# Order of shifts and scores within a head attention step

## The chip, the cores and the metric

The kernel runs on one core of a Trainium2 chip. The time is device time in microseconds of one execution. TensorE (PE) does the matrix products, ScalarE (ACT) the exponentials and copies, VectorE (DVE) maxima and sums, GpSimd (POOL) sums of pairs and casts, SyncE (SP) issues the transfers.

## The reference

Eight batch elements, each with 1024 rows of 512 numbers and a context of 1024 rows of 384. Two gated residual blocks follow each other; the first is cross attention with 8 heads of 64 (here: kind 1), the second self attention with 16 heads of 32 and a gate on each row (kind 2).

```python
q = (x @ Wq).reshape(B, Nq, HEADS, DIM_HEAD)             # kind 1, k and v from the context
sim = jnp.einsum('bihd,bjhd->bhij', q, k) * SCALE
attn = jax.nn.softmax(sim, axis=-1)
out = jnp.einsum('bhij,bjhd->bihd', attn, v)
...
q_scaled = (q_norm + query_embedding[None]) * jax.nn.softplus(temperature)[None]   # kind 2
attn = jnp.einsum('bhqd,bhkd->bhqk', q_scaled, k) / math.sqrt(hd)
attn = jax.nn.softmax(attn, axis=-1)
h = jnp.einsum('bhqk,bhkd->bhqd', attn, v)
...
x = x + jnp.tanh(g_xattn[0]) * _L0_xattn_ref(_layernorm(x), ...)
x = x + jnp.tanh(g_ffn[0]) * _L0_ffn_ref(_layernorm(x), ...)
```

## The kernel before

Batch elements are worked one after the other. For each element and kind the heads go in four chunks of 128 rows (class `Chunk`): two heads of 64 rows in kind 1, four heads of 32 rows in kind 2. The rows of q and k that belong to one head sit on that head's rows of TensorE's array, so the products of different heads of a chunk use different row groups.

A chunk passes through three stages, which overlap with those of its neighbours. `project` makes q and k. `maxima` (L373) computes scores once in bf16 into tiles `pm` and takes their row maxima on VectorE (L421, or L404 where two banks go at once); the negated maxima are turned to rows `sh` by a transfer. `attention` (L590) then goes over the steps (h, s): h is one half of 512 queries, s runs over four pairs of key blocks (kind 1) or eight key blocks (kind 2). With four chunks, two halves and eight elements there are 256 steps of kind 1 and 512 of kind 2.

A step is made by `score` (L445) and `value` (L549). `score` fills two PSUM tiles `sc` of two banks each, so four banks in all. Bank j gets two products, summed in PSUM: the shift, a product of a row of ones with a row of `sh` (m == 0, bf16, one row of the array), and the score, k times q (m == 1, fp32). In kind 2 the four banks belong to the four heads, on four different row groups: tile 0 has heads 0 and 1, tile 1 heads 2 and 3. ScalarE then takes the exponential of each tile into a tile `e` (L473). `value` multiplies `e` with v into the tile `av` (L560); these products use all rows of the array and 32 or 64 of its columns. GpSimd and VectorE add up `e` tiles (L478, L491) for the sums (L511).

The pool `ps_sc` has two buffers, so a step's tile can be written only when the exponential of the step before has read the same buffer. The score of step m + 1 is issued before the value of step m. The variable `order` says which tile comes first; in kind 2 it is turned round when the maxima pair just issued (`taken`) uses the rows of heads 0 and 1:

```python
order = (1, 0) if taken[0] and self.kind == 2 else (0, 1)
...
for m in range(2):
    for j in (2 * u + v for u in order for v in range(2)):
```

[...]`attend` (L679) fills in maxima and projections between scores and values by planned times (`pe`, `dve`, `pool`, with `self.SC` 1250 ns for a kind-2 score step). These planned times don't depend on the order within `score`.

Of the kernel before, what the change touches and what calls it, by code (L numbers as in the profile page):

```python
# [21 lines left out]
def tile_gated_block(  # L22
# [38 lines left out]
    nc = tc.nc  # L61
# [172 lines left out]
    def pe(ns):  # L234
        at["PE"] += ns
# [27 lines left out]
    class Chunk:  # L263
# [181 lines left out]
        def score(self, step):  # L445

            h, s = step
            nh, width, key = self.nh, self.width, self.key  # L450
            order = (1, 0) if taken[0] and self.kind == 2 else (0, 1)
            taken[0] = False
            pss = {
                u: ps_sc.tile([P, 2, H], F32, tag="sc", name=f"sc_{key}_{h}_{s}_{u}") for u in order
            }
            for m in range(2):
                for j in (2 * u + v for u in order for v in range(2)):
                    kk, i = divmod(j, nh)
                    r, kc = i * width, s * self.nk + kk
                    if m == 0:  # L460
                        r += kk * HD2
                        lhsT, rhs = ones_b[r : r + 1, :], self.sh[r : r + 1, ts(h, H)]
                    else:
                        rows = slice(r, r + width)
                        lhsT, rhs = self.k[rows, ts(kc, P)], self.q[rows, ts(h, H)]
                    nc.tensor.matmul(  # L466
                        pss[j // 2][:, j % 2, :], lhsT=lhsT, rhs=rhs, start=(m == 0), stop=(m == 1)
                    )
            pe(self.SC)
            e = {}  # L470
            for u in order:
                e[u] = epool.tile([P, 2, H], F32, tag="e", name=f"e_{key}_{h}_{s}_{u}")
                nc.scalar.activation(e[u], pss[u], AF.Exp)  # L473
            self.e[step] = e
# [639 lines left out]
```

## Time and profile before

| | |
|---|---|
| median of 3 runs | 4967.27 us (4964.01 to 4967.46) |
| profiled execution | 4964.66 us, span 4962.6 us |
| granted TensorE clock | 0.998 |
| TensorE busy | 4751.6 us (96%) |
| VectorE busy | 3126.6 us (63%) |
| GpSimd busy | 2571.3 us (52%) |
| ScalarE busy | 2307.6 us (47%) |
| scores sc<-q,k L466 | 6144 matmuls, 1114.5 us busy |
| shifts sc<-sh,ones_b L466 | 3072 matmuls, 408.2 us busy, 99.9 us idle before |
| exponentials e<-sc L473 | 1536, 1491.1 us busy, mean 1021 ns |

A line of the timeline gives the start and length in us of neighbouring instructions of one kind, the engine, the line of the kernel, what is written and read, how many, and in brackets the engine's idle time before them with what ended it. PEld are TensorE's weight loads. A matmul's end is modelled: its row is longer than the time for which it holds its rows of the array, so starts are compared with starts. A wait for several semaphores is put down to the one that came last.

### The profile page before, as it was taken

Reading aid. Unit: us, or ns where it says so; the run is one execution under the profiler, and the core shown is the slowest. Engines: PE = TensorE matmul, PEld = TensorE weight load, DVE = VectorE, ACT = ScalarE, POOL = GpSimd, SP = SyncE. Lnnn points to the kernel's source line nnn. Section 1 sums busy time; section 2 is a strip of 40 time slices with the busy share of each in tenths; the row PEclk is TensorE's granted clock in tenths of the full one; section 3 lists DMA queues with packets and bytes.
Section 4 is the critical chain, followed back from the end, with each engine's and each line's share of the span. In section 5 each row is a group of like instructions: output and inputs, shape, how many; then the busy total and the mean of one; then the engine's idle time right before and its main releaser. Section 6 shows DMA issues by size and latency. Waiting matters only on the chain.

```text
span 4962.6 us, 83502 instructions
## 1 busy us (share of the span) xinstructions
PE 4751.6 (96%) x35476; PEld 1413.5 (28%) x35476; DVE 3126.6 (63%) x4148; ACT 2307.6 (47%) x3029; POOL 2571.3 (52%) x1346
## 2 busy tenths in 40 slices
PE   9999999999999999999999999999999999999988
PEld 2222232222322223222232222322223222232222
DVE  5557765577655775557755577555775557754664
ACT  3435634356343563435634356243562436624354
POOL 1635646366463663636636366363663636636464
PEclk9999999999999999999999999999999999999999
DMA  2010010100101001010010100201001010010000
GB/s 80 26 33 15 25 50 26 34 16 24 50 26 37 13 24 50 26 37 13 24 64 12 37 13 23 65 11 37 13 26 64 10 37 18 13 52 5 23 1 18
DMA packets 126277, 145.14 MB, mean 29 GB/s; under 512 B 14544, under 2 KB 75984, under 8 KB 125904
## 3 DMA queue, kind: packets, MB, share of 16 engines
q1 hardware_dynamic: 125616, 139.81, 8.9%
q8 instruction: 277, 4.54, 0.4%
q14 instruction: 96, 0.79, 0.1%
q10 hardware_dynamic: 288, 0.00, 0.0%
HBM read 122.47 MB, written 16.78 MB: 28 GB/s over the span
## 4 chain that ended last, share of the span: by engine, by line
PE 78%; DVE 10%; ACT 6%; issue 3%; POOL 2%; DMA 0%; SPq 0%; ACTq 0%; DVEq 0%; POOLq 0%
PE sc L466 20%; PE av L560 16%; PE po L249 8%; PE pq L249 8%; PE pk L249 7%; PE pm L380 7%; PE pv L249 6%; DVE mx L404 4%; ACT e L473 4%; PE sum L511 3%; DVE mx L421 3%; DVE e L491 2%; POOL e L478 2%; PE pt L218 1%; PE pn L249 1%
## 5 line engine op out<-in xcount | busy, mean ns | idle before, releaser
L478 POOL TENSOR_TENSOR e<-e,e 128x1024 f32<-128x1024 f32 x764 | 1863.5, 2454 | 1248.7 <-PE av L560 647.5
L473 ACT ACTIVATE e<-sc 128x1024 f32<-128x1024 f32 x1536 | 1491.1, 1021 | 1278.8 <-PE sc L466 1255.8
L421 DVE TENSOR_REDUCE mx<-pm 128x1 f32<-128x512 f32 x2332 | 1494.1, 685 | 807.2 <-PE pm L380 793.1
L466 PE MATMUL sc<-q,k 32*128 32x512 f32 (+1 forms) x6144 | 1114.5, 604 | 0.0
L491 DVE TENSOR_TENSOR e<-e,e 128x1024 f32<-128x1024 f32 x477 | 897.7, 1900 | 319.0 <-POOL e L478 317.4
L560 PE MATMUL av<-e,v 128*32 128x512 f32 (+1 forms) x6144 | 1074.5, 608 | 0.0
L380 PE MATMUL pm<-kb,qb 32*128 32x512 bf16 (+1 forms) x3072 | 621.7, 382 | 47.4 <-DVE mx L404 25.2
L404 DVE TENSOR_REDUCE mx<-pm 128x2 f32<-128x1024 f32 x370 | 427.8, 1219 | 292.3 <-PE pm L380 292.3
L466 PE MATMUL sc<-sh,ones_b 1*128 1x512 bf16 x3072 | 408.2, 383 | 99.9 <-ACT e L473 87.2
L466 PEld LDWEIGHTS sc<-q,k 32*128 32x128 f32 (+1 forms) x6144 | 419.4, 186 | 188.7 <-issue 180.9
L380 PEld LDWEIGHTS <-qb 32*128 32x128 bf16 (+1 forms) x3072 | 146.2, 91 | 922.0 <-issue 897.8
L560 PEld LDWEIGHTS av<-e,v 128*32 128x32 f32 (+1 forms) x6144 | 193.5, 117 | 607.0 <-issue 579.2
L249 PE MATMUL pq<-y1T,wq 128*32 128x512 f32 (+1 forms) x1568 | 248.3, 599 | 5.8 <-ACT k L335 2.5
L249 PE MATMUL pk<-y2T,wk 128*32 128x512 f32 x2048 | 241.3, 595 | 7.4 <-ACT qq L322 7.4
L249 PE MATMUL pq<-y2T,wq 128*32 128x512 f32 x2048 | 244.9, 595 | 2.8 <-ACT rn L347 2.8
L249 PE MATMUL pv<-wv,y2T 128*32 128x512 f32 x2048 | 241.3, 597 | 0.0
L466 PEld LDWEIGHTS <-ones_b 1*128 1x128 bf16 x3072 | 101.8, 91 | 467.3 <-issue 450.7
L249 PE MATMUL po<-wp,h2T 128*64 128x512 f32 (+1 forms) x1152 | 231.1, 595 | 0.0
L249 PE MATMUL po<-wo,h1T 128*32 128x512 f32 x2048 | 229.7, 594 | 1.2 <-ACT y2T L219 0.5
L249 PE MATMUL pk<-ctx,wk 128*32 128x512 f32 (+1 forms) x1176 | 190.2, 603 | 17.5 <-ACT r L535 8.6
L349 POOL TENSOR_TENSOR qq<-qq,rn 128x512 f32<-128x512 f32 x64 | 88.3, 1380 | 220.6 <-ACT rn L348 220.6
L249 PE MATMUL pv<-wv,ctx 128*32 128x512 f32 x1536 | 194.2, 596 | 5.4 <-ACT v L793 5.4
(109 smaller groups left out, 2848.8 us busy)
## 6 DMA issues: line engine op xcount, KB each, us to landing
x<-in_x SPq DMA_DIRECT2D x64, 256.0 KB
out<-x SPq DMA_DIRECT2D x64, 256.0 KB
xs<-in_x SPq DMA_DIRECT2D x56, 256.0 KB
xn<-in_x SPq DMA_DIRECT2D x56, 256.0 KB
ctx<-in_ctx SPq DMA_DIRECT2D x7, 1536.0 KB
wq<-in_L_xattn_Wq SPq DMA_DIRECT2D x32, 256.0 KB
wo<-in_L_xattn_Wo SPq DMA_DIRECT2D x8, 1024.0 KB
wk<-in_L_ffn_Wk SPq DMA_DIRECT2D x32, 256.0 KB
```

The costliest lines, as they stand in the source:

```text
L218: nc.tensor.transpose(pt[:, c, :], xn[:, ts(c, P)], ident)
L249: nc.tensor.matmul(ps[ts(j, w), :], lhsT=lhsT[:, ts(j, w)], rhs=rhs, start=start, stop=stop)
L349: nc.gpsimd.tensor_tensor(self.qq, self.qq, rn, ALU.mult)
L380: nc.tensor.matmul(ps, lhsT=self.qb[ts(i, width), ts(c, P)], rhs=self.kb[ts(i, width), ts(kh, H)], start=True, stop=True,)
L404: nc.vector.tensor_reduce(out, tiles[u], AX.X, ALU.max)
L421: nc.vector.tensor_reduce(mx[:, i * NT + c, kh : kh + 1], ps, AX.X, ALU.max)
L466: nc.tensor.matmul(pss[j // 2][:, j % 2, :], lhsT=lhsT, rhs=rhs, start=(m == 0), stop=(m == 1))
L473: nc.scalar.activation(e[u], pss[u], AF.Exp)
L478: nc.gpsimd.tensor_tensor(one, one, two, ALU.add)
L491: nc.vector.tensor_tensor(accs[-1], accs[-1], a, ALU.add)
L511: nc.tensor.matmul(ps[ts(2 * u + j, self.width), :], lhsT=ones[:, 0 : self.width], rhs=acc[n][:, j, :], start=(n == 0), stop=(n == len(acc ...
L560: nc.tensor.matmul(self.av[ts(i, width), :], lhsT=st.v[:, kc, ts(self.c * self.nh + i, width)], rhs=e[j // 2][:, j % 2, :], start=(kc == 0 ...
```

## The change

In `score` the loop over the four banks becomes a function `products(m, u)` for the two banks of tile u. In kind 2 both products (shift, then score) of the first tile in `order` are issued, then both of the other tile. In kind 1 the shifts of both tiles are issued and then the scores of both, as before.

```diff
-            for m in range(2):
-                for j in (2 * u + v for u in order for v in range(2)):
+
+            def products(m, u):
+                for j in (2 * u, 2 * u + 1):
                     kk, i = divmod(j, nh)
                     r, kc = i * width, s * self.nk + kk
                     if m == 0:
...
-                    nc.tensor.matmul(
-                        pss[j // 2][:, j % 2, :], lhsT=lhsT, rhs=rhs, start=(m == 0), stop=(m == 1)
-                    )
+                    nc.tensor.matmul(pss[u][:, j % 2, :], lhsT=lhsT, rhs=rhs, start=(m == 0), stop=(m == 1))
+
+
+            for half in [order] if self.kind == 1 else [order[:1], order[1:]]:
+                for m in range(2):
+                    for u in half:
+                        products(m, u)
             pe(self.SC)
```

So a kind-2 step with order (0, 1) issues shift 0, shift 1, score 0, score 1, shift 2, shift 3, score 2, score 3, where it issued shifts 0 to 3 and then scores 0 to 3.

## The prediction

> **What bounds the kernel now.** I read the page's shares first, then its groups for the changed line, then the waits of TensorE, then the timeline of single steps. The profiled execution took 4964.66 us (span 4962.6); the runs' median is 4967.27.
>
> ```profile
> PE 4751.6 (96%) x35476; PEld 1413.5 (28%) x35476; DVE 3126.6 (63%) x4148; ACT 2307.6 (47%) x3029; POOL 2571.3 (52%) x1346
> PE 78%; DVE 10%; ACT 6%; issue 3%; POOL 2%; DMA 0%; SPq 0%; ACTq 0%; DVEq 0%; POOLq 0%
> L466 PE MATMUL sc<-q,k 32*128 32x512 f32 (+1 forms) x6144 | 1114.5, 604 | 0.0
> L466 PE MATMUL sc<-sh,ones_b 1*128 1x512 bf16 x3072 | 408.2, 383 | 99.9 <-ACT e L473 87.2
> ```
>
> TensorE is busy nearly throughout, so only what shortens TensorE's own sequence counts. The columns of a group are busy us, mean ns of one, and idle us before it with its releaser. The shifts on L466 are the one large group with idle time that ScalarE ends; the 3072 score products stand as 6144 matmuls, because each fp32 product is two matmuls, one behind the other in TensorE's stream.
>
> ```profile
> PE sc L466 <- ACT e L473: 87.2, 161, 3.7
> PE pm L380 <- DVE mx L404: 25.2, 92, 0.5
> PE sc L466 <- DMA sh<-rows: 11.1, 22, 2.5
> ```
>
> This is the list of TensorE's waits (us in total, times, longest). The first is the largest of the program: a shift waits until an exponential has read the PSUM tile that the shift overwrites. Sorting the records of L466 by step: 138 of these waits, 73.8 us, fall on the second pair of shifts of a kind-2 step (32-row scores), about 10 us on kind 1, the rest on first pairs. The pairs follow each other 0.00 us apart in 229 of the 512 kind-2 steps, about 0.2 us apart in some 130 (a maxima pair on the same rows goes first), and 0.71 to 0.91 us apart in the 138. The recorded 0.5 us understates a stall, since a shift's row lasts 0.39 us.
>
> One stalled step, TensorE, then ScalarE:
>
> ```profile
> 2960.05 0.39 PE L380 MATMUL pm<-kb,qb 32*128 32x512 bf16 x2
> 2960.05 0.39 PE L466 MATMUL sc<-sh,ones_b 1*128 1x512 bf16 x2
> 2960.94 0.39 PE L466 MATMUL sc<-sh,ones_b 1*128 1x512 bf16 x2 [0.50 <-ACT e L473]
> 2960.95 1.24 PE L466 MATMUL sc<-q,k 32*128 32x512 f32 x8
> 2961.91 0.38 PE L380 MATMUL pm<-kb,qb 32*128 32x512 bf16 x2
> 2962.22 1.07 PE L560 MATMUL av<-e,v 128*32 128x512 f32 x8
> 2963.22 0.39 PE L466 MATMUL sc<-sh,ones_b 1*128 1x512 bf16 x2
> ```
>
> ```profile
> 2958.95 1.94 ACT L473 ACTIVATE e<-sc 128x1024 f32<-128x1024 f32 x2 [1.23 <-PE sc L466]
> 2962.12 1.94 ACT L473 ACTIVATE e<-sc 128x1024 f32<-128x1024 f32 x2 [0.53 <-PE sc L466]
> ```
>
> The old exponentials end at 2960.89; 0.05 us later the second shifts start, and only with them all scores, those of the first tile too, whose shifts had been done since 2960.3. So the first exponential starts 1.18 us after the second shifts, the pair takes 1.94, and 0.05 later the next second shifts go: a loop of 3.17 us a step, while TensorE's own way from second shifts to the next first shifts is 2.28.
>
> And a step without a stall (TensorE, then its weight loads, then ScalarE):
>
> ```profile
> 3064.54 0.39 PE L466 MATMUL sc<-sh,ones_b 1*128 1x512 bf16 x4
> 3064.76 1.03 PE L466 MATMUL sc<-q,k 32*128 32x512 f32 x8
> ```
>
> ```profile
> 3064.55 0.41 PEld L466 LDWEIGHTS sc<-q,k 32*128 32x128 f32 x8
> ```
>
> ```profile
> 3065.89 1.94 ACT L473 ACTIVATE e<-sc 128x1024 f32<-128x1024 f32 x2 [2.07 <-PE sc L466]
> ```
>
> A shift holds its rows 0.22 us (3064.54 to 3064.76), one half of a score 0.44 (1.03 less the 0.59 of one matmul), four row groups at once. Shifts to first exponential: 1.35 us.
>
> **The change, part by part.** Nothing is added or removed: the same 12 matmuls a step, the same exponentials, planner costs and DMAs. Kind 1 keeps its order exactly, so 256 of 768 steps can't move. In the 512 kind-2 steps the scores of the first tile move ahead of the second tile's shifts.
>
> *The stalled steps.* The first tile's scores no longer stand behind the wait. Let a and b be the starts of the first and second shifts. The first exponential then starts at a + 1.35 instead of b + 1.18, both are done at a + 3.29, and the next b can be at a + 3.34. The stalled step itself gains nearly nothing: the value products need all rows, so they wait for the second scores, which end where they did (b + 1.1). Only a maxima pair that stood ahead of them (77 of the 138) now runs under the wait: value products 0.1 us sooner, b to next a 2.18. What is gained is the next step. With maxima: a0 = 0, b0 = 0.89; a1 = 0.89 + 2.18 = 3.07; b1 = 3.34, a wait of 0.27 instead of 0.89; a2 = 3.34 + 2.22 = 5.56 (the pair now runs under only part of the wait); b2 = 3.07 + 3.34 = 6.41, a wait of 0.85 again. So stalls alternate: two steps take 5.56 instead of 6.34, saving 0.78. Without maxima (2.25 from b to a in the trace): 3.16, then 5.59, saving 0.75.
> The 138 stalls stand in 66 runs of neighbouring steps: 37 of one, 2 of two, 18 of three, 7 of four, one of six and one of nine. Every second place of a run gains: 2 + 18 + 14 + 3 + 4 = 41, four in each of the first seven batch elements, 13 in the last. 41 x 0.77 = **31.6 us**. The 0.1 us of single stalls with maxima (about 35) adds 3.5.
> What is late next: in such a run VectorE has four maxima of 0.65 us a step, 2.61, under the new mean of 2.78 with three buffers between, so it doesn't bind; it would bind from 2.61 on, so no further gain hides there.
>
> *The unstalled steps.* Here the second shifts now stand behind the first tile's four score matmuls. The rows are different, so they can start at once if TensorE lets them past. The stream puts both halves of a product before the next product, yet the rows show eight half products in 1.03 us, four at a time: first halves of the later products overtake waiting second halves of earlier ones. The weight loads say more: by the records the first-half loads of all four products start within 0.02 us of 3064.55, while the shifts still run, the fourth past nine waiting instructions. The moved shifts have six before them (four matmuls and two second loads) plus two loads already under way. So I cost them at the issue alone, 7 ns a product by the same records: 0.014 x 229 = 3.2 us. Where maxima hold the rows for 0.2 us anyway it is hidden. If that cover fails, it costs what the second rival gives.
> *The rule against it.* The Trainium skill, TensorE: Matmul & The Clock Gate (Part 3: Packing small matmuls, The mechanism), has matmuls strictly in program order in start and end, with only weight loads pulled ahead. By that rule the second shifts start with the last second half, 0.65 us late in 229 steps and 0.44 in 130: 149 + 57 = 206 us lost. But by the same rule the eight matmuls above would take five slots of 0.44 and a tail, over 2 us; the row has 1.03. I take the row. Strict order among matmuls of different rows is not what this trace shows.
>
> Sum: 31.6 + 3.5 - 3.2 = 32, of which I leave 1 to waits that come later: 31. On the profiled execution's own time 4964.7 - 31 = 4933.7; on the median, 2.6 above it, **4936 us** (-0.6%). Bounds of the gain: 20 if a third is taken up by later waits (VectorE's maxima, ScalarE's other work at 0.8 us a piece in some runs), 42 if the stall evens out with the maxima hidden in every run.
>
> **Rivals.** *Nothing to gain (no change):* the stalls move instead of vanishing, as they do in the 37 single ones; if the 41 did likewise, because ScalarE's first exponential is released only with both tiles' scores, 4964 to 4970. Against it: in steps with shifts 0.2 us apart the first exponential starts 1.30 after the first shifts, not 1.35 after the second.
> *Matmuls are not let past a product that waits twice (slower):* a row group may hold one waiting matmul only. Then the second half of the first score stops the stream until the shift ends, and the moved shifts start 0.22 late in the 229 unstalled steps without maxima: +50, less 31, **4986**; by the full rule +206 - 31, about 5140. It decides from 31 / 229 = 0.14 us a step on. For it: I found no row in which a matmul (rather than a weight load) starts past a matmul that isn't a second half. Against it: the loads do, and a matmul follows its load.
>
> **How the numbers follow.** Gain as worked out 0.72 (4925 to 4949); no change 0.10 (4958 to 4977); held shifts 0.18 (0.10 near 4986, 0.08 near 5140). Two tenths of a per cent, 10 us, is about what a measurement tells from no change. So faster 0.72, same 0.10, slower 0.18. The range for 8 in 10 takes the gain with tails, no change and half of the milder loss: 4920 to 4990.
>
> **What would show it.** Right: the waits of L466 for e fall from 87 us to some 60, with shorter ones between long ones in runs of stalls, such a run alternating steps of about 3.1 and 2.45 us; unstalled steps as long as before. Wrong: second shifts 0.2 us or more behind the first with no wait named, eight scores no longer within 1.03 us, or stalls of 0.9 us in every step of a run.

## The result and the profile after

The changed kernel takes 4949.19 us (median of 6 runs, 4946.06 to 4951.34) against 4967.47 (median of 6, with later runs of it): a ratio of 0.9965, 95% interval 0.9955 to 0.9976. It is 18.3 us faster where 31 were forecast. Its profiled execution took 4946.06 us (span 4944.0, 18.6 below the kernel before). Lines behind the edit have moved: L467 is L466 of before, L478 the exponentials (L473), L483 GpSimd's pair sums (L478), L496 VectorE's running sums (L491).

The page's shares and the two groups of the changed line, after:

```profile
PE 4799.9 (97%) x35476; PEld 1447.5 (29%) x35476; DVE 3136.0 (63%) x4148; ACT 2309.7 (47%) x3029; POOL 2589.9 (52%) x1346
L467 PE MATMUL sc<-q,k 32*128 32x512 f32 (+1 forms) x6144 | 1193.2, 599 | 0.0
L467 PE MATMUL sc<-sh,ones_b 1*128 1x512 bf16 x3072 | 407.4, 383 | 31.4 <-ACT e L478 20.1
```

The same instructions, and TensorE's busy time is 48 us *longer*. Scores that used to stand still behind a wait now run two at a time while the other two wait, so the group's covered time grows from 1114.5 to 1193.2 us with a slightly shorter mean. A recorded idle gap has become a half-used array. That is why TensorE's list of waits (us in total, times, longest) now overstates the success:

```profile
PE sc L467 <- ACT e L478: 20.1, 31, 2.9
PE sc L467 <- DMA sh<-rows: 10.9, 21, 1.8
PE pm L380 <- DVE mx L421: 10.5, 47, 0.4
```

It says 67 us less waiting for exponentials; the span says 18.6. Of the delays themselves, the distance between the two pairs of shifts within a step, 112 are still above 0.4 us (138 before; in both kernels one more, of about 4 us, stands in the last chunk).

A run of stalls after the change, TensorE then ScalarE:

```profile
2951.65 0.39 PE L467 MATMUL sc<-sh,ones_b 1*128 1x512 bf16 x2
2951.87 0.59 PE L467 MATMUL sc<-q,k 32*128 32x512 f32 x2
2951.89 0.39 PE L467 MATMUL sc<-sh,ones_b 1*128 1x512 bf16 x2
...
2953.11 1.06 PE L565 MATMUL av<-e,v 128*32 128x512 f32 x8
...
2954.11 0.39 PE L467 MATMUL sc<-sh,ones_b 1*128 1x512 bf16 x2
2954.34 1.02 PE L467 MATMUL sc<-q,k 32*128 32x512 f32 x4
2954.93 0.39 PE L467 MATMUL sc<-sh,ones_b 1*128 1x512 bf16 x2
...
2956.11 1.06 PE L565 MATMUL av<-e,v 128*32 128x512 f32 x8
```

```profile
2952.94 1.94 ACT L478 ACTIVATE e<-sc 128x1024 f32<-128x1024 f32 x2 [0.41 <-PE sc L467]
2955.41 1.94 ACT L478 ACTIVATE e<-sc 128x1024 f32<-128x1024 f32 x2 [0.53 <-PE sc L467]
```

The step at 2951.65 has its second shifts 0.24 us behind the first; the one at 2954.11 waits 0.82 for them, but its first tile's scores run meanwhile, so its first exponential starts 1.30 us after the *first* shifts. In the kernel before, both of these steps stalled 0.88. The step starts of this run are 3.05, 2.46 and 4.72 us apart, where they were 3.15, 3.17 and 4.88: the forecast alternation.

An unstalled step after:

```profile
3058.13 0.41 PE L467 MATMUL sc<-sh,ones_b 1*128 1x512 bf16 x4
3058.36 1.04 PE L467 MATMUL sc<-q,k 32*128 32x512 f32 x8
```

Four shifts within 0.41 us and eight scores within 1.04 (0.39 and 1.03 before). The second shifts start 0.017 us behind the first in the median of the unstalled steps (0.003 before). The step itself got no longer by that: over the 222 steps in which neither kernel has the pairs more than 0.1 us apart, the last score starts 0.013 us later, but the median difference in length, start to start, is 0.000.

So where did 13 us go? Step by step (start to start, kind 2 within one batch element), the steps that got shorter sum to 36.9 us and those that got longer to 18.2. Of the longer ones, 9.7 us stand where an exponential now waits for a sum, or waits longer for it than before. ScalarE's waits by releaser, before and then after:

```profile
ACT e L473 <- DVE e L491: 20.0, 19, 3.0
ACT e L473 <- POOL e L478: 0.7, 1, 0.7
```

```profile
ACT e L478 <- DVE e L496: 56.0, 38, 3.9
ACT e L478 <- POOL e L483: 5.7, 6, 1.3
```

An exponential can't start before one of the nine `e` buffers is free, and a buffer is free when its sum (GpSimd adds pairs, VectorE adds pairs to a running total) has read it. These waits grew from 20.7 to 61.7 us, of which 36 fall on kind-2 steps. Two of them, on TensorE, ScalarE and VectorE:

```profile
3036.69 0.39 PE L467 MATMUL sc<-sh,ones_b 1*128 1x512 bf16 x2
3036.91 1.03 PE L467 MATMUL sc<-q,k 32*128 32x512 f32 x4
3038.10 0.39 PE L467 MATMUL sc<-sh,ones_b 1*128 1x512 bf16 x2 [0.16 <-ACT e L478]
```

```profile
3037.02 1.02 ACT L478 ACTIVATE e<-sc 128x1024 f32<-128x1024 f32 x1 [0.38 <-DVE e L496]
3039.00 1.94 ACT L478 ACTIVATE e<-sc 128x1024 f32<-128x1024 f32 x2 [0.95 <-DVE e L496]
```

```profile
3033.57 5.34 DVE L496 TENSOR_TENSOR e<-e,e 128x1024 f32<-128x1024 f32 x2 [4.04 <-POOL e L483]
3041.15 3.37 DVE L496 TENSOR_TENSOR e<-e,e 128x1024 f32<-128x1024 f32 x1 [2.25 <-POOL e L483]
```

By its single records, VectorE's first sum ends at 3036.93 and frees the buffer for the exponential at 3037.02, the second ends at 3038.90 for the one at 3039.00. The second shifts come 1.41 us behind the first; the usual stall before was 0.88, and only the one in the last chunk was longer than this.

There is a second way, which doesn't pass through the `e` buffers. VectorE also takes the maxima, and these queue up behind its sums. One kind-2 step, the same in each of the first seven elements, got longer by 0.57 to 0.86 us, 4.4 us in all, and no exponential waits for a buffer there. VectorE's two sums and TensorE's maxima products in the fifth element, before:

```profile
2911.45 2.76 DVE L491 TENSOR_TENSOR e<-e,e 128x1024 f32<-128x1024 f32 x2
2917.93 0.39 PE L380 MATMUL pm<-kb,qb 32*128 32x512 bf16 x2
```

And after:

```profile
2902.55 5.83 DVE L496 TENSOR_TENSOR e<-e,e 128x1024 f32<-128x1024 f32 x2
2908.30 2.47 DVE L421 TENSOR_REDUCE mx<-pm 128x1 f32<-128x512 f32 x4
2909.03 0.38 PE L380 MATMUL pm<-kb,qb 32*128 32x512 bf16 x1
2909.63 0.37 PE L380 MATMUL pm<-kb,qb 32*128 32x512 bf16 x1 [0.22 <-DVE mx L421]
```

The step starts at 2914.68 before and at 2905.78 after, so the sums begin 3.23 us ahead of it in both. But they now take 5.83 us instead of 2.76, the maxima behind them come late, and the second maxima product starts 0.60 us behind the first instead of with it. The pair sum of GpSimd that runs beside these sums ends 0.9 us later against the step than before.

### The profile page after: what moved, and what is told of

Read it like the earlier page. It is cut to its first block, busy times and chain, and to the rows that moved or that the text cites. A ratio compares the mean times of both kernels' runs of the same rounds, so it can differ in the third digit from the quotient of the medians.

```text
span 4944.0 us, 83502 instructions
## 1 busy us (share of the span) xinstructions
PE 4799.9 (97%) x35476; PEld 1447.5 (29%) x35476; DVE 3136.0 (63%) x4148; ACT 2309.7 (47%) x3029; POOL 2589.9 (52%) x1346
## 4 chain that ended last, share of the span: by engine, by line
PE 80%; DVE 12%; ACT 3%; issue 3%; POOL 2%; DMA 0%; SPq 0%; DVEq 0%; ACTq 0%; POOLq 0%
PE sc L467 21%; PE av L565 17%; PE po L249 8%; PE pq L249 7%; PE pm L380 7%; PE pk L249 7%; PE pv L249 6%; DVE mx L404 4%; DVE e L496 3%; DVE mx L421 3%; PE sum L516 3%; POOL e L483 2%; ACT e L478 1%; PE pt L218 1%; PE pn L249 1%
## 5 line engine op out<-in xcount | busy, mean ns | idle before, releaser
L483 POOL TENSOR_TENSOR e<-e,e 128x1024 f32<-128x1024 f32 x764 | 1881.3, 2477 | 1222.5 <-PE av L565 618.6
L478 ACT ACTIVATE e<-sc 128x1024 f32<-128x1024 f32 x1536 | 1493.2, 1021 | 1237.9 <-PE sc L467 1174.7
L467 PE MATMUL sc<-q,k 32*128 32x512 f32 (+1 forms) x6144 | 1193.2, 599 | 0.0
L496 DVE TENSOR_TENSOR e<-e,e 128x1024 f32<-128x1024 f32 x477 | 909.8, 1926 | 319.5 <-POOL e L483 318.0
L467 PEld LDWEIGHTS sc<-q,k 32*128 32x128 f32 (+1 forms) x6144 | 480.2, 188 | 196.7 <-issue 185.4
L467 PE MATMUL sc<-sh,ones_b 1*128 1x512 bf16 x3072 | 407.4, 383 | 31.4 <-ACT e L478 20.1
L467 PEld LDWEIGHTS <-ones_b 1*128 1x128 bf16 x3072 | 103.3, 91 | 403.9 <-issue 389.6
```

The costliest lines, as they stand in the source:

```text
L467: nc.tensor.matmul(pss[u][:, j % 2, :], lhsT=lhsT, rhs=rhs, start=(m == 0), stop=(m == 1))
L483: nc.gpsimd.tensor_tensor(one, one, two, ALU.add)
L496: nc.vector.tensor_tensor(accs[-1], accs[-1], a, ALU.add)
```

## The experiments

The theory after the result: the split opens the loop as worked out, and the exponentials, now earlier, run into `e` buffers that the sums still hold. Rivals: the give-back is TensorE's own (order, PSUM), or the layer norm's buffers and transfers.

**One more e buffer.** The room for the tenth buffer is taken elsewhere:

```diff
-epool = ctx.enter_context(tc.tile_pool(name="epool", bufs=9))
+epool = ctx.enter_context(tc.tile_pool(name="epool", bufs=10))
-xn = work.tile([P, D], F32, tag="wa", ..., bufs=4)          # and in load_rows
+xn = work.tile([P, D], F32, tag="wa", ..., bufs=3)
-lg = ... tag=f"lg{h}"; m8 = ... tag=f"m8{h}"
+lg = ... tag="lg"; m8 = ... tag="m8"
```

> The changed kernel with a tenth buffer for the exponentials' tiles (pool e), paid for by three instead of four buffers for the rows read for the first layer norm, and one tile instead of two for the gates' logits and for their maxima. Theory A (the 18 us that the change gives back go to exponentials that wait for an e buffer, which sums on VectorE and GpSimd still hold): the exponentials' waits for those sums fall from 61.7 us to under 20, and the time to 4933 to 4939, 10 to 16 below the changed kernel. Theory B (the sums themselves are too slow, one more buffer only moves the wait a step on): waits of 45 us and more, time within 4 us of the changed kernel's 4949.

> The kernel before with the same tenth e buffer and the same three tiles. Theory A: the kernel before waits 20.7 us for e buffers on ScalarE, of which little lies on TensorE's path, so it gains 1 to 5 us: 4962 to 4966; the change on top of it (against the changed kernel with ten buffers) is then worth 25 to 32 us instead of 18. Theory B: the difference between the two stays at 18 to 20.

Measured: 4928.11 us with the change (ratio to the kernel before 0.9926, 0.9913 to 0.9938) and 4955.62 without (0.9980, 0.9971 to 0.9989). The changed kernel gains 21 us from the buffer, more than the 16 at most that I had given it; the kernel before gains 10, twice the most that I expected. By step, 9 of these 10 lie in kind 1, which I hadn't looked at. Between the two stand 27.5 us instead of 18.3, within the 25 to 32 of theory A. ScalarE's list of the changed kernel with ten buffers:

```profile
ACT e L478 <- DVE e L496: 14.5, 11, 2.9
ACT e L478 <- DVE mv L199: 13.0, 6, 2.2
ACT e L478 <- POOL e L483: 1.5, 2, 0.8
```

The waits for sums fall to 16. The middle line is new; I put it down to the three buffers of the layer norm. By step, 43.4 us are now gained and 11.8 given back, so the buffer helps but isn't the whole of it: the seven steps with late maxima are still longer, by 0.63 to 0.65 us each, 4.5 in all. At 4928 us this version is also the fastest of this study with nothing left out, level with the one that is paid for by the weights' buffers below.

**What paid for it, alone, and paid for by something else.**

```diff
-xn = work.tile([P, D], F32, tag="wa", ..., bufs=4)          # after_w3: only this, in both places
+xn = work.tile([P, D], F32, tag="wa", ..., bufs=3)
...
-w = wpool.tile([P, ap.shape[0] // P, P], F32, tag="wc", name=name, bufs=4)    # after_wc3: this
+w = wpool.tile([P, ap.shape[0] // P, P], F32, tag="wc", name=name, bufs=3)    # with ten e buffers
```

> The changed kernel with nothing of the tenth e buffer but the three (instead of four) buffers for the rows of the first layer norm that paid for it. If the gain of the ten-buffer version is the e buffer's, this one is not faster than the changed kernel: 4948 to 4958. If it were the layer norm's buffers (fewer transfers in flight beside the sums), it would be near 4930.

> The changed kernel with ten e buffers, paid for by three instead of four buffers for the projections' weights, and one tile each for the gates' logits and their maxima; the layer norm keeps its four. Exponentials wait 13 us for the layer norm's statistics in the version paid for there; if that wait is on TensorE's path, this one is 4 to 8 us faster than 4928: 4920 to 4924. If the weights then come late (a product that waits for its weights after the load that had to wait for a buffer), 4930 to 4945.

Measured: 4948.21 us with the layer norm's three buffers alone, no different from the changed kernel, so the gain is the e buffer's. With the weights' buffers as payment 4928.60, between my two forecasts and no different from 4928.11, and its list has the same line `DVE mv L199: 13.0, 6, 2.2`. My reading of that line was wrong: neither is it due to the layer norm's buffers (it is there with four) nor did taking three of the weights' cost anything. It shows up only with ten e buffers, for a cause that I didn't follow further.

**Half of the sums left out.** With the same instructions over 256 of 512 queries, a sum takes about half as long (VectorE's 0.68 us at best instead of 1.21, GpSimd's 1.27 in the median instead of 2.36). Half of each sum is left out in these kernels.

```diff
-nc.gpsimd.tensor_tensor(one, one, two, ALU.add)
+nc.gpsimd.tensor_tensor(one[:, :, 0:256], one[:, :, 0:256], two[:, :, 0:256], ALU.add)
...
-nc.vector.tensor_tensor(accs[-1], accs[-1], a, ALU.add)
+nc.vector.tensor_tensor(accs[-1][:, :, 0:256], accs[-1][:, :, 0:256], a[:, :, 0:256], ALU.add)
```

> The kernel before, with the sums of exponentials (the pair sum on GpSimd and the running sum on VectorE) over only 256 of the 512 queries of each bank: half of each sum is left out. Same instructions, about half as long. Both theories: ScalarE's waits for e buffers go, 4955 to 4966; the stalls of the second shifts stay, about 138 of 0.9 us.

> The changed kernel with the same halves of the sums left out. If the holding of e buffers by these sums, of whichever cause, took back the 18 us, the change is worth its whole predicted gain here: 30 to 37 us below the kernel before with the same halves, 4922 to 4934. If the give-back has another cause (TensorE's order, PSUM), the difference stays at 18 to 20 us.

Measured: 4937.85 us without the change and 4893.83 with it. The kernel before gains far more (27.6 us below its 4965.43 on the same chip) than I gave it, by step 15.6 us of it in kind 1. With the sums out of the way the change is worth 44.0 us, more than the 30 to 37 that I expected. The one wait of an exponential for a sum that is left in the changed one:

```profile
ACT e L478 <- DVE e L496: 1.2, 1, 1.2
```

By step 44.8 us are gained and 6.3 given back. Outside of these, seven times 0.8 us is gained between the last kind-2 step of an element and the first of the next: the last kind-2 step stalls, and the first kind-1 step behind it was the one that waited. Together 44.8 - 6.3 + 5.6 = 44.1. This decides against a give-back by TensorE's order or by PSUM: neither is different here. With whole sums the same seven places came out at -0.8 to +0.8, sum about 0. The seven steps with late maxima are 5.45 us long here with and without the change, so that loss was the sums' too. Only the tenth buffer parts it from the loss by the `e` buffers: with that one it stays.

**Which engine's sums.** Only one of the two edits above each, on the changed kernel; half of that engine's sums is left out.

> The changed kernel, pair sums on GpSimd over 256 of the 512 queries of each bank (half of these sums is left out), running sums on VectorE whole. Theory P (GpSimd sets when an e buffer comes free, both by its own time and by slowing VectorE's sums that run beside it): VectorE's sums of 3.4 us become rare, the exponentials' waits for e buffers fall from 61.7 us to under 15, time 4893 to 4912. Theory V (VectorE's sums set it): waits of 30 us and more, 4930 to 4945.

> The changed kernel, running sums on VectorE over 256 of the 512 queries of each bank (half of these sums is left out), pair sums on GpSimd whole. Theory P: waits for e buffers stay above 25 us, 4932 to 4944. Theory V: they fall under 15 us, 4893 to 4912.

Measured: 4900.27 us with GpSimd's halved, waits for e buffers 2.7 us, as theory P had it; 4913.38 with VectorE's halved, waits 16.9 us, which fits neither (P wanted over 25, V under 15 and a time up to 4912). Both engines hold the buffers, GpSimd more. Neither edit was run on the kernel before, so this tells what limits the changed kernel, not how the 13 us divide. The group of VectorE's untouched sums shows one reason why GpSimd weighs more, first in the changed kernel, then with GpSimd's sums halved:

```profile
L496 DVE TENSOR_TENSOR e<-e,e 128x1024 f32<-128x1024 f32 x477 | 909.8, 1926 | 319.5 <-POOL e L483 318.0
```

```profile
L496 DVE TENSOR_TENSOR e<-e,e 128x1024 f32<-128x1024 f32 x477 | 658.7, 1399 | 302.6 <-POOL e L483 301.6
```

The same 477 instructions take 1926 ns beside full pair sums and 1399 beside half ones. In the changed kernel a sum takes 1.21 us at best, and 80 of the 477 take over 3, like the one at 3041.15 above: by the single records a pair sum of GpSimd runs from 3041.08 to 3043.44, and the next, begun at 3043.39, takes 3.34 us instead of 2.36. With half pair sums no running sum takes over 2.31. The Trainium skill has this: SBUF — State Buffer, SBUF: two separate sides, says that a VectorE operation with two inputs in SBUF and a GpSimd operation that reads SBUF lock a shared pair of ports for the whole instruction, and the later one is blocked. By that rule a sum of 1.21 us that meets a pair sum of 2.36 takes up to 3.57; the rows show at most 3.38.

**The split in kind 1 too.**

```diff
-for half in [order] if self.kind == 1 else [order[:1], order[1:]]:
+for half in [order[:1], order[1:]]:
```

> The changed kernel with the same split in kind 1 too. There a tile's two heads take 64 rows each, so the first tile's scores hold all four row groups, and the second tile's shifts cannot pass them. If free row groups are what makes the split free of cost, each of the 256 kind-1 steps gets longer by a shift's 0.22 us, about 56 us in all, less at most the 10 us of stalls in kind 1: 4995 to 5010. If matmuls pass each other whatever rows they use, or the split costs nothing anyway, 4935 to 4952.

Measured: 5062.61 us (ratio to the kernel before 1.0197, 1.0180 to 1.0214), 113 us above the changed kernel. The direction is the one forecast for shared rows, the size is twice the price. A kind-1 step, before and with the split:

```profile
2700.83 0.40 PE L466 MATMUL sc<-sh,ones_b 1*128 1x512 bf16 x4
2701.15 1.99 PE L466 MATMUL sc<-q,k 64*128 64x512 f32 x8
2703.07 1.08 PE L560 MATMUL av<-e,v 128*64 128x512 f32 x4
```

```profile
2697.24 0.39 PE L467 MATMUL sc<-sh,ones_b 1*128 1x512 bf16 x2
2697.56 1.13 PE L467 MATMUL sc<-q,k 64*128 64x512 f32 x4
2698.62 0.39 PE L467 MATMUL sc<-sh,ones_b 1*128 1x512 bf16 x2
2698.94 1.13 PE L467 MATMUL sc<-q,k 64*128 64x512 f32 x4
2700.00 1.08 PE L565 MATMUL av<-e,v 128*64 128x512 f32 x4
```

First shift to value products: 2.24 us becomes 2.76, here and in the median of the 256 kind-1 steps. Shifts hold 0.32 us before scores of 64 rows (0.22 before scores of 32), and the second shifts start 1.06 us behind the first scores, which hold their rows only 0.88 (the second half starts 0.44 after the first). I read this as a turn between products on 32 and on 64 rows that costs 0.1 to 0.2 us beside the shift, of which the split makes two more: 0.22 + 0.10 + 0.18 is 0.50 of the 0.51. No run changes the rows alone, so that the turn is the cause isn't shown. Shifts with no free rows wait for the scores; shifts with free rows, as in kind 2, pass them in 0.017 us.

## Why the prediction was right, and where it was off

*The number.* The range held, but by its width: the gain of 18.3 us is below the 20 that I gave as its lower bound, and 4949.19 stands just outside the 4925 to 4949 of the outcome that I held most likely.

*The bound and the loop.* Right. TensorE's sequence decides, the 3.17 us loop was closed by the second shifts standing before the first scores, and it opens as worked out: 0.82 and 0.24 us in place of 0.88 and 0.88.

*The stalled step itself.* Right: in the 99 steps that stall in both kernels the value products start 0.10 us sooner after the first shifts, in the median.

*41 second places at 0.77, and 3.5 for single stalls.* 35.1 us forecast, 36.9 measured as the sum of the shortened kind-2 steps. That the two agree is partly luck. Of the second places, 33 came out (a stall before and none after), at 0.71 us each in the median, 23.8 us together instead of 31.6; steps that stall in both kernels gave 8.7 instead of 3.5; the other 4.4 are steps that weren't in the sum. With ten e buffers 40 come out and with the sums halved 43, again at 0.71 each, so the count was right for a kernel whose sums aren't in the way, and the size was a little too high. (Without maxima the first step of two is 3.14 us by its own terms, not 3.16; the saving stands.) The working missed the stall behind the last kind-2 step of an element, which the first kind-1 step pays: up to 5.6 us more, seen only with the sums halved.

*The unstalled steps.* The delay is right to the nanosecond that the records give: 0.014 us forecast, 0.017 less 0.003 measured. As a cost it was too high: 3.2 us were charged, and the median of these steps got no longer. Strict program order among matmuls would have shown the second shifts 0.65 us late; the split in kind 1 shows what they cost once rows are shared.

*"32, of which I leave 1 to waits that come later".* This term failed: 1 us was left for later waits, and by step 18.2 were given back. I did name VectorE's maxima as a later wait, but judged them by their own 2.61 us a step, without the sums that they stand behind: that cost the 4.4 us of the seven steps above, of which TensorE's list shows only 2 (8.5 to 10.5). A third of the gain, my bound, was too little. What I passed over was the pool of the exponentials' tiles: earlier exponentials ask for their buffers earlier, while the sums that free them go no faster. The 20 us of ScalarE's waits for sums were there to be read in the profile before, and so was GpSimd: in the chain of eight stalls in the last element it was busy 21.34 of 24 us (4686 to 4710 us of the kernel before). That is an estimated 2.82 us for a step of 3.17, so steps of 2.78 had to run into it. Not every longer step is explained by these two. In the last chunk of the last element four steps got longer by 0.4 to 1.0 us, in part where shifts wait for their rows `sh`; these I didn't take apart.

*What would show it.* I expected TensorE's waits for exponentials at some 60 us; they are 20, because a wait beside running scores leaves no idle gap. The sign was badly chosen: the distance between the shifts is the thing to read.

*The rivals.* Neither came true. The exponential is released by its own tile's scores (1.30 us after the first shifts while the second stand 0.82 behind), and the second shifts do pass scores that still wait.

## What to carry to other kernels

When products on separate row groups wait for different buffers, issue each group's whole sequence before the other group's wait; with free rows this delayed the second shifts by 0.014 us here and left the median step as long as it was, with shared rows it cost 0.51 us a step. Before pricing such a gain, follow the buffer that the sped-up engine writes to the engines that free it, and ask whether they have time left in just that stretch, and what else queues behind them: with the sums halved the change was worth 44 us instead of 18, and one more tile in the pool gave about as much as the change itself. A wait that vanishes from the list of an engine's idle time may only have moved beside half-used work, so count time from step to step.

## What the runs showed that I had not expected

One e buffer more gave about 20 us to the changed kernel, as much as the change did (21 by the medians above; 19.6 between the layer norm's three buffers alone and the ten buffers paid for by the weights', which ran on one chip). VectorE's running sums of the same shape took from 1.2 to 3.4 us, depending on whether GpSimd's pair sums ran beside them. Shifts and 64-row scores that alternate cost 0.1 to 0.2 us at each turn, on top of what they stream, for a cause that isn't shown.
